# Layer 1 of a graph network: TensorE in written order around the maximum, ten pairs of values ahead of the first product, both last sums of layer 0 ahead of their norms

## The chip, the cores and the metric

The kernel runs on one core of a Trainium2 chip. The metric is the device time of one execution in microseconds (us), lower is better. The core has five engines with a queue each: TensorE (PE in the profile, its weight loads PEld), VectorE (DVE), ScalarE (ACT), GpSimd (POOL) and SyncE (SP), which here issues nearly all DMAs.

## The reference, cut to what matters

Four layers work on 3125 nodes of 128 values and 103125 edges; each ends with `x = layernorm(x + layer(x))`.

```python
x = _layernorm(x + _L0_gnn_ref(...))   # relu(segment_sum(w * (x @ W)[src], dst) + b)
x = _layernorm(x + _L1_gnn_ref(...))   # attention over edges, 4 heads of 32 values
x = _layernorm(x + _L2_gnn_ref(...))   # attention with q, k, v
x = _layernorm(x + _L3_gnn_ref(...))   # two mean aggregations
```

Layer 1, for each head, with h = x @ W:

```python
a_s = einsum('nhc,hc->nh', h, att_src); a_d = einsum('nhc,hc->nh', h, att_dst)
e = leaky_relu(a_s[src] + a_d[dst], 0.2)
p = exp(e - segment_max(e, dst)[dst]); z = segment_sum(p, dst)
out = segment_sum(h[src] * (p / z[dst]), dst) + gat_bias + x @ skip_W + skip_b   # then a layer norm
```

## The kernel before

The graph is turned into dense matrices of 25 x 25 blocks of 128 x 128: the summed edge weights in DRAM as `wd` (f32), the edge counts as `ctd` (bf16). Gathers and segment sums are then products on TensorE.

**Layer 0.** For each of 25 blocks i of source nodes, `adds0` (L840) loads the block row of `wd` with SyncE (`cw`, L847) and records products with `xw` (L851). `rows` and `todo` add the first 20 destination blocks (Z0 = 20) into five banks `acc0`. The other five blocks go into two banks, `left0` (four blocks) and `left1` (one), `acc1` in the program: rows 0 to 5 early (L1024), and rows 6 to 24 (ZA = 6) as "left rows", by `add0` (L857) in the loop `for i in range(NB)`. `end0` (L861) closes a bank: one sum with relu (L863), then the layer norm (L816): four bn_stats (L822), four aggregates (L824), small steps, a root on ScalarE (L827) and four scalings on ScalarE (L833).

**The start of layer 1.** While the left rows are summed, the finished blocks are prepared in groups of four:
- `scores1(g)` (L1280) transposes the group (`turned`, four transposes, L1042), copies it to `xT` (ScalarE L546 or VectorE L548, in turn), multiplies with the attention vectors per block (`tr_sa`, L1287) and for the row of destination scores (`tr_ad`, L1294); ScalarE copies this row out (L1296) and SyncE stores it in DRAM (L1297).
- `top` (L1401) takes the maximum of the source scores over the first eight blocks: `heads` copies the scores (L1303), a transpose on TensorE (`few`, L1076), a reduction and a small step on VectorE, and a second product on TensorE that spreads it over the partitions (L1085). From it `factors` makes the exponentials (ScalarE L1317 to L1320).
- `values(b)` (L1336) makes the values of one pair of blocks: two products (`trw`, L1341), two multiplications on VectorE (L1346), a split into three bf16 parts (`split3`, L562: VectorE L566 and L568, three casts on ScalarE, L564, L567 and L569), and a negation (L1357) into `vp`. The products `trw` use two banks in turn. `more_values` (L1407) calls it for the next pair.

The dictionary `marks` says in which step i of the loop which of these is recorded. Eight pairs (blocks 0 to 15) and the masks of column blocks 0, 1 and 2 are recorded in the loop.

**The products of layer 1.** `items` runs over two groups of destination blocks (12 and 13), four heads and 25 column blocks c. `masks` (L1370) loads the counts `ct` (L1380) and makes the mask `cm`: mostly a relu on ScalarE (L1388) and a minimum on VectorE (L1392), for some c one step on VectorE (L1384). `products` (L1456) issues two matmuls for each destination block: counts (L1464) and mask (L1468) with `vp`. A block c needs its values and its mask. The six accumulators of a head include the banks of `left0` and `left1`. The remaining pairs are recorded in this loop, as c comes near them (`ready <= c + 4`).

**What sets the order.** Each engine works through its own queue in order. Where the program says nothing, a scheduler at build time interleaves the recorded instructions by priority. `tc.manual_schedule(engines=...)` keeps the recorded order on the engines it names for the instructions recorded inside it, while the scheduler may still put others between them. `tc.issue_after(ins)` places what is recorded inside it behind `ins`, on the same engine. In the loop over `items`, the masks made in the first three steps stand behind `added`, the last sum of layer 0 (`end0` returns it).

Of the kernel before, what the change touches and what calls it, by code (L numbers as in the profile page):

```python
# [13 lines left out]
OP = mybir.AluOpType  # L14
# [486 lines left out]
ZA = 6  # L501
# [18 lines left out]
def fast_path(  # L520
# [4 lines left out]
    nc = tc.nc  # L525
# [9 lines left out]
    x = cst.tile([P, NB, P], F32, name="f_x")  # L535
# [37 lines left out]
    lp0 = ctx.enter_context(tc.tile_pool(name="f_lp0", bufs=2))  # L573
# [242 lines left out]
    def layer_norm(lp, o, i, blocks, scalar=False):  # L816

        b0, n = blocks
        bs = lp.tile([P, n, 6], F32, name="bs")
        mv = lp.tile([P, n, 2], F32, name="mv")  # L820
        for b in range(n):
            nc.vector.bn_stats(bs[:, b, :], i[:, b0 + b, :])  # L822
        for b in range(n):
            nc.vector.bn_aggr(mv[:, b, :], bs[:, b, :])  # L824
        sd = lp.tile([P, n], F32, name="sd")
        nc.vector.tensor_scalar(sd, mv[:, :, 1], EPS, None, OP.add)
        nc.scalar.activation(sd, sd, AF.Sqrt)  # L827
        nc.vector.reciprocal(sd, sd)
        if scalar:
            ms = lp.tile([P, n], F32, name="ms")  # L830
            nc.vector.scalar_tensor_tensor(ms, mv[:, :, 0], -1.0, sd, OP.mult, OP.mult)
            for b in range(n):
                nc.scalar.activation(  # L833
                    o[:, b0 + b, :], i[:, b0 + b, :], AF.Identity, bias=ms[:, b : b + 1], scale=sd[:, b : b + 1]
                )
            return
        for b in range(n):
            nc.vector.tensor_scalar(o[:, b0 + b, :], i[:, b0 + b, :], mv[:, b, 0:1], sd[:, b : b + 1], OP.subtract, OP.mult)
# [18 lines left out]
    def add0(*args):  # L857
        for f in adds0(*args):
            f()

    def end0(acc, b0, n):  # L861
        i = x[:, b0 : b0 + n, :]
        added = nc.vector.scalar_tensor_tensor(i, acc[:, 0:n, :], 0.0, i, OP.max, OP.add)  # L863
        layer_norm(lp0, i, i, (0, n), True)
        return added

    zp = front.enter_context(tc.tile_pool(name="f_zp", bufs=4))
    sp = front.enter_context(tc.tile_pool(name="f_stg", bufs=2))
# [63 lines left out]
    order = None  # L932
# [4 lines left out]
    for b in range(NBT):  # L937
# [65 lines left out]
        if b == 2:  # L1003
# [4 lines left out]
            order = ExitStack()  # L1008
# [3 lines left out]
    left = GB[Z0 // 4 :]  # L1012
    acc1 = [zpp.tile([P, 4, P], F32, name=f"left{k}") for k in range(len(left))]
# [241 lines left out]
    with ExitStack() as st:  # L1255
# [21 lines left out]
        for g in range(Z0 // 4):  # L1277
            end0(acc0[g], *GB[g])
# [28 lines left out]
        def factors(b0, n):  # L1307
            b = slice(b0, b0 + n)
            kb = km[:, None, :].to_broadcast([P, n, H])
            ta = fp.tile([P, NB, H], F32, name="ta", bufs=1)[:, 0:n]  # L1310
            nc.vector.tensor_tensor(ta, sa[:, b, 0:H], kb, OP.subtract)
            u = fp.tile([P, NB, H], F32, name="u", bufs=1)[:, 0:n]
            nc.vector.tensor_tensor(u, sa[:, b, H:], kb, OP.add)
            e = fp.tile([P, 2, NB, H], F32, name="e", bufs=1)[:, :, 0:n]
            nc.vector.tensor_scalar(e[:, 0], u, 0.8, 0.0, OP.mult, OP.min)
            nc.vector.tensor_scalar(e[:, 1], u, -0.8, 0.0, OP.mult, OP.min)
            nc.scalar.activation(fa[:, 0, b], ta, AF.Exp)  # L1317
            nc.scalar.activation(fa[:, 1, b], ta, AF.Exp, scale=0.2)
            nc.scalar.activation(own1[:, b], ta, AF.Exp, scale=-0.8)
            nc.scalar.activation(fb[:, :, b], e, AF.Exp)  # L1320
            nc.vector.tensor_scalar(fa[:, 1, b], fa[:, 1, b], -1.0, None, OP.mult)

            nc.vector.tensor_tensor(own1[:, b], own1[:, b], fb[:, 1, b], OP.mult)
            nc.vector.tensor_tensor(own1[:, b], own1[:, b], fb[:, 0, b], OP.max)
            nc.gpsimd.tensor_tensor(self_[:, b, :, C], own1[:, b], fa[:, 0, b], OP.mult)
            split3(
                fp, lambda k: of_v(b, k).rearrange("p a (s c) -> p a s c", c=F1)[:, :, :, C],
                fa[:, :, b].rearrange("p s b h -> p (b h) s"), [P, n * H, 2], "fs", [P, 12 * H, 2],
            )
            v = vp[:, b].rearrange("p b h k c -> p (b h) k c")  # L1330
            nc.vector.tensor_scalar(v[:, :, :, 2 * F1 + C], v[:, :, :, F1 + C], -1.0, None, OP.mult)
# [4 lines left out]
        def values(b):  # L1336

            n = min(2, NB - b)
            t = zps.tile([P, 2, P], F32, name="trw2", tag=f"acc{b // 2 % 2}")
            for k in range(n):  # L1340
                nc.tensor.matmul(t[:, k, :], xT[:, (b + k) * P : (b + k + 1) * P], l1_wt, start=True, stop=True)  # L1341
            h_ = t[:, 0:n].rearrange("p b (h c) -> p b h c", c=C)
            b = slice(b, b + n)
            v = fp.tile([P, 2, H, 2, C], F32, name="v")[:, 0:n]
            for s in range(2):
                nc.vector.tensor_tensor(  # L1346
                    v[:, :, :, s, :], h_, fa[:, s, b, :, None].to_broadcast([P, n, H, C]), OP.mult
                )
            nc.gpsimd.tensor_tensor(
                self_[:, b, :, 0:C], v[:, :, :, 0, :], own1[:, b, :, None].to_broadcast([P, n, H, C]), OP.mult,  # L1350
            )
            split3(
                fp, lambda k: of_v(b, k).rearrange("p a (s c) -> p a s c", c=F1)[:, :, :, 0:C],
                v.rearrange("p b h s c -> p (b h) s c"), [P, n * H, 2, C], "vs", [P, 2 * H, 2, C],
            )
            v = vp[:, b].rearrange("p b h k c -> p (b h) k c")
            nc.vector.tensor_scalar(v[:, :, :, 2 * F1 : 2 * F1 + C], v[:, :, :, F1 : F1 + C], -1.0, None, OP.mult)  # L1357
# [12 lines left out]
        def masks(g, h, c):  # L1370
            i0, n = IG[g]
            if c == 0:
                adr = dp.tile([P, GN * P], F32, name="adr")
                nc.sync.dma_start(
                    adr[:, : n * P],
                    bass.AP(tensor=add_.tensor, offset=add_.offset + h * NP + i0 * P, ap=[[0, P], [1, n * P]]),
                )
                adrs[g, h] = adr
            ct = cp.tile([P, GN * P], BF16, name="ct1")
            nc.sync.dma_start(ct[:, : n * P], ctd[c, :, i0 * P : (i0 + n) * P])  # L1380
            m = mp.tile([P, GN * P], BF16, name="cm")
            if c % 5 == 4 and (h == 0 or c == 14):
                with behind_sum(c):
                    pins["v"] = nc.vector.scalar_tensor_tensor(  # L1384
                        m[:, : n * P], adrs[g, h][:, : n * P], nas[:, c, h : h + 1], ct[:, : n * P], OP.is_gt, OP.mult
                    )
            else:
                pins["a"] = nc.scalar.activation(  # L1388
                    m[:, : n * P], adrs[g, h][:, : n * P], AF.Relu, bias=bas[:, c, h : h + 1], scale=UP
                )  # L1390
                with behind_sum(c):
                    pins["v"] = nc.vector.tensor_tensor(m[:, : n * P], m[:, : n * P], ct[:, : n * P], OP.min)  # L1392
            whole = not (h > 0 and c % 5 == 1)
            if not whole:
                pins["v"] = nc.vector.tensor_tensor(ct[:, : n * P], ct[:, : n * P], m[:, : n * P], OP.subtract)  # L1395
            ready_[g, h, c] = (ct, m, whole)
# [10 lines left out]
        def more_values():  # L1407
            nonlocal ready
            values(ready)
            ready += 2  # L1410
# [8 lines left out]
        marks[ZA + 6] = lambda: scores1(4)  # L1419
        marks[ZA + 7] = lambda: (more_values(), heads(t8, 8, Z0 - 8))  # L1420
        marks[ZA + 8] = lambda: factors(8, Z0 - 8)
        for i in (15, 17, 20, 22):
            marks[i] = more_values
        for i in range(NB):
            if i >= ZA:
                add0(cp, i, acc1, (Z0, NB - Z0), "ct1")
            if i in marks:
                marks[i]()
            if i in (19, 21, 23):
                masks(*items[(i - 19) // 2])  # L1430
# [3 lines left out]
        later(7, lambda: factors(Z0, NB - Z0))  # L1434

        for g, (b0, n) in enumerate(left):
            added = end0(acc1[g], b0, n)

        def in_range():

# [101 lines left out]
        acc = None  # L1542
        for x_, (g, h, c) in enumerate(items):
            i0, n = IG[g]
            if c == 0:
                acc = [zps.tile([P, 512], F32, name="acc1", tag=f"acc{k}") for k in ((3, 4, 2), (0, 3, 4, 2))[g]]
# [107 lines left out]
    with ExitStack() as st:  # L1654
# [108 lines left out]
        acc = None  # L1763
        for x_, (q, c) in enumerate(items):
            i0, n = QG[q]
            if c == 0:
                acc = [ap.tile([P, 512], F32, name=f"acc2_{k}") for k in range((n + 2) // 3)]
# [51 lines left out]
    with ExitStack() as st:  # L1819
# [7 lines left out]
        for g in range(3, len(GB)):  # L1827
            b0, n = GB[g]
# [3 lines left out]
        acc = [ap.tile([P, 512], F32, name=f"acc3_{k}") for k in range(len(CN))]  # L1832
# [64 lines left out]
        for k in range(K + 3):  # L1897
            if k < K:
                c, n = CN[k]
# [221 lines left out]
```

## Time and profile before

| what | value |
|---|---|
| median of 3 runs | 1296.39 us (1295.44 to 1298.28) |
| profiled execution | 1297.9 us |
| its span, first to last instruction | 1296.1 us |
| mean granted TensorE clock | 0.99 |
| TensorE busy | 1232.1 us, 95% of the span |
| VectorE busy | 955.0 us, 74% |
| ScalarE busy | 864.9 us, 67% |

Times in lines of the profile are microseconds from the start of the span. A line of a timeline has the start, the duration, the engine, the line of the program, the operation, out<-in, the shape and how many; in brackets the idle time before it and what ended it. A line of windows has, for each engine, the busy time and the number of instructions, then the granted TensorE clock, the DMA share and GB/s. An f32 matmul appears as two MATMUL records. A busy TensorE need not be at its peak, since matmuls are pipelined.

### The profile page before, as it was taken

To read this page: it belongs to the slowest core of one execution; us is meant where nothing else is said; L and a number is where in the kernel's file an instruction comes from. 1 tells how busy PE (TensorE), PEld (TensorE's weight loads), DVE (VectorE), ACT (ScalarE), POOL (GpSimd) and SP (SyncE) were. 2 spreads that over 40 slices of the span, in tenths; PEclk is the share of its full clock that TensorE was granted. 3 is DMA by queue.
4 is the path that set the end of the run, shared out by engine and by line. 5 is a ranking of instruction groups with operands and counts; after the bars stand their busy time and mean duration, and the time that the engine had idled before them with its cause. 6 is when DMAs were issued, how large, how long until landed. Compare 5 with 4: busy or idle time off the path is not lost.

```text
span 1296.1 us, 31070 instructions
## 1 busy us (share of the span) xinstructions
PE 1232.1 (95%) x13022; PEld 1100.1 (85%) x13022; DVE 955.0 (74%) x1461; ACT 864.9 (67%) x1374; POOL 149.4 (12%) x161
## 2 busy tenths in 40 slices
PE   3989999999999999999999999999999999999996
PEld 3889999999998889999999897777787778876785
DVE  6989989999925998998999987944464437332365
ACT  2977778787744997998789886534474444543454
POOL 6100000000002212230223232000000000000011
PEclk9999999999999999999999999999999999999999
DMA  7589899998997767888878775522222223861674
GB/s 186 144 234 285 240 266 279 281 275 258 286 306 248 265 197 230 281 281 257 274 252 264 210 253 190 179 74 64 62 78 74 77 63 114 262 194 49 208 209 146
DMA packets 189347, 262.37 MB, mean 202 GB/s; under 512 B 10604, under 2 KB 132763, under 8 KB 189069
## 3 DMA queue, kind: packets, MB, share of 16 engines
q1 hardware_dynamic: 188172, 257.85, 65.2%
q8 instruction: 104, 1.70, 0.5%
q0 software_dynamic: 720, 1.97, 0.5%
q10 hardware_dynamic: 305, 0.48, 0.2%
q14 instruction: 46, 0.38, 0.1%
HBM read 197.14 MB, written 63.12 MB: 201 GB/s over the span
## 4 chain that ended last, share of the span: by engine, by line
PE 69%; DVE 12%; DMA 8%; ACT 6%; issue 3%; POOL 1%; SPq 1%; POOLq 0%; ACTq 0%; DVEq 0%
PE acc L1731 9%; PE acc L1468 9%; PE s L1723 8%; PE wp L960 8%; PE acc L851 7%; PE acc L1464 5%; PE acc L1836 5%; DMA wd<-ws 5%; PE cp L952 4%; PE acc L1918 4%; DVE cm L1392 3%; ACT cm L1388 2%; DMA ct<-f_ctd 2%; DVE e L1727 1%; ACT wod L741 1%
## 5 line engine op out<-in xcount | busy, mean ns | idle before, releaser
L1464 PE MATMUL acc<-vp,ct 128*128 128x99 bf16 (+1 forms) x2500 | 323.4, 209 | 7.1 <-DVE vp L1357 5.2
L1468 PE MATMUL acc<-vp,cm 128*128 128x198 bf16 (+1 forms) x2500 | 325.2, 244 | 2.3 <-DVE cm L1392 2.0
L1388 ACT ACTIVATE cm<-adr,bas 128x1536 bf16<-128x1536 f32 (+1 forms) x184 | 287.2, 1619 | 28.5 <-PE acc L1468 19.9
L1468 PEld LDWEIGHTS <-cm 128*128 128x128 bf16 x2500 | 240.2, 97 | 13.4 <-issue 8.7
L1464 PEld LDWEIGHTS <-ct 128*128 128x128 bf16 x2500 | 242.7, 98 | 1.2 <-DVE ct L1395 0.8
L1392 DVE TENSOR_TENSOR cm<-cm,ct 128x1536 bf16<-128x1536 bf16 (+1 forms) x184 | 199.4, 1109 | 21.4 <-ACT cm L1388 19.8
L1726 ACT ACTIVATE e<-s,f_nm 128x512 f32<-128x512 f32 (+2 forms) x175 | 109.7, 633 | 114.9 <-PE s L1723 110.5
L1727 DVE TENSOR_TENSOR e<-e,ct 128x512 f32<-128x512 f32 (+2 forms) x175 | 107.7, 622 | 99.4 <-ACT e L1726 94.5
L960 PE MATMUL wp<-wod,ohc 128*128 128x128 f16 x2512 | 168.8, 220 | 2.4 <-DVE wod L908 2.2
L1731 PEld LDWEIGHTS acc<-self__6345,e 128*128 128x128 f32 x1250 | 147.5, 192 | 19.4 <-issue 10.5
L908 DVE TENSOR_TENSOR wod<-ohd,w 128x4096 f16<-128x4096 f16 (+1 forms) x82 | 155.6, 1939 | 0.0
L960 PEld LDWEIGHTS <-ohc 128*128 128x128 f16 x2512 | 150.1, 99 | 0.9 <-issue 0.3
L851 PE MATMUL acc<-f_xw,cw 128*128 128x128 f32 x1000 | 145.3, 286 | 2.8 <-DMA cw<-wd 2.8
L1731 PE MATMUL acc<-self__6345,e 128*128 128x129 f32 x1250 | 147.8, 275 | 0.0
L1723 PE MATMUL s<-yT,f_xT 128*128 128x512 f32 (+2 forms) x350 | 140.2, 538 | 1.2 <-DVE f_xT L548 1.1
L851 PEld LDWEIGHTS acc<-f_xw,cw 128*128 128x128 f32 x1000 | 125.5, 195 | 3.2 <-DMA cw<-wd 3.2
L1645 ACT CAST cr<-ct 128x1590 fp32r<-128x1590 bf16 (+3 forms) x51 | 72.3, 1418 | 77.5 <-PE acc L1836 38.1
L741 ACT COPY ws<-wp 125x512 f32<-125x512 f32 x157 | 91.2, 581 | 43.4 <-DMA wd<-ws 33.7
L741 ACT CAST cs<-cp 128x500 bf16<-128x500 f32 x157 | 91.5, 583 | 29.8 <-PE cp L952 23.8
L952 PE MATMUL cp<-ohc,ohd 128*128 128x125 f16 x1256 | 96.2, 220 | 11.6 <-ACT ws L741 11.5
L1723 PEld LDWEIGHTS s<-yT,f_xT 128*128 128x128 f32 x350 | 62.9, 190 | 49.6 <-issue 20.8
L741 ACT ACTIVATE wod<-ohd,wt 128x128 f16<-128x128 f16 x312 | 104.6, 401 | 0.0
(349 smaller groups left out, 1518.7 us busy)
## 6 DMA issues: line engine op xcount, KB each, us to landing
ct<-f_ctd SPq DMA_DIRECT2D x186, 384.0 KB
ct<-f_ctd SPq DMA_DIRECT2D x100, 416.0 KB
wd<-ws SPq DMA_DIRECT2D x39, 896.0 KB
cw<-wd SPq DMA_DIRECT2D x50, 640.0 KB
f_ctd<-cs SPq DMA_DIRECT2D x10, 2000.0 KB
ct<-f_ctd SPq DMA_DIRECT2D x25, 397.2 KB
ct<-f_ctd SPq DMA_DIRECT2D x22, 397.5 KB
ct<-f_ctd SPq DMA_DIRECT2D x25, 269.5 KB
```

The source lines that it names most:

```text
L741: line.append(f(*a, **k))
L851: steps.append(lambda j=j, a=cw[:, j - h, :]: nc.tensor.matmul(accs[j // 4][:, j % 4, :], a, xw[:, i, :], start=(i == 0 and j % 4 == 0), s ...
L908: tip[s] = nc.vector.tensor_tensor(packed(f, ww), packed(ohd, ww), twos(w2[s])[:, ww], OP.mult)
L952: nc.tensor.matmul(cp[:, j, 0:KW], ohd[:, w, :], ohc[:, w, 0:KW], start=(j == 0 and q == 0), stop=(j == 3 and q == 1), skip_group_check=True,)
L960: tip["made"] = made = nc.tensor.matmul(wp[:, j, :], ohc[:, w, :], wod[s][:, w, :], start=(j == 0 and q == 0 and s == 0), stop=(j == 3 and ...
L1388: pins["a"] = nc.scalar.activation(m[:, : n * P], adrs[g, h][:, : n * P], AF.Relu, bias=bas[:, c, h : h + 1], scale=UP)
L1392: pins["v"] = nc.vector.tensor_tensor(m[:, : n * P], m[:, : n * P], ct[:, : n * P], OP.min)
L1464: nc.tensor.matmul(out_(F1, w), ct[:, k * P : (k + 1) * P], vp[:, c, h, :, 2 * F1 : F1 + w], start=(c == 0 and k % 2 == 0), stop=False, sk ...
L1468: pins["p"] = nc.tensor.matmul(out_(0, z), m[:, k * P : (k + 1) * P], vp[:, c, h, :, 0:z], start=False, stop=(c == NB - 1 and (k % 2 == 1 ...
L1723: nc.tensor.matmul(s[:, :m], xT[:, c * P : (c + 1) * P], yT[:, i0 * P + a : i0 * P + a + m], start=True, stop=True)
L1727: masked2.append(nc.vector.tensor_tensor(e[:, a : a + m], e[:, a : a + m], ct[:, a : a + m], OP.mult))
L1731: nc.tensor.matmul(acc[k // 3][:, (k % 3) * (P + 1) : (k % 3 + 1) * (P + 1)], es[q, c][:, k * P : (k + 1) * P], vo[:, c, 0 : P + 1], start ...
```

## The change

Three things are changed, and no arithmetic. The steps i = ZA - 1 to ZA + 3 of the loop (the scores of groups 0 and 1, the maximum, the first factors, the first two pairs, the scores of group 2, and four left rows) are recorded under `manual_schedule` for TensorE. Pairs of values are recorded in steps 19, 21 and 23 instead of 20 and 22, and one more behind the last sum, so that ten pairs instead of eight stand ahead of the first product. The sum of `end0` becomes a function `add_acc`; the two sums of `left0` and `left1` come first, and both layer norms after them. `added` is still the sum of `left1`.

```diff
     def end0(acc, b0, n):
         i = x[:, b0 : b0 + n, :]
-        added = nc.vector.scalar_tensor_tensor(i, acc[:, 0:n, :], 0.0, i, OP.max, OP.add)
+        add_acc(acc, b0, n)
         layer_norm(lp0, i, i, (0, n), True)
-        return added
+
+    def add_acc(acc, b0, n):
+        i = x[:, b0 : b0 + n, :]
+        return nc.vector.scalar_tensor_tensor(i, acc[:, 0:n, :], 0.0, i, OP.max, OP.add)
...
-        for i in (15, 17, 20, 22):
+        for i in (15, 17, 19, 21, 23):
             marks[i] = more_values
+        order = ExitStack()
         for i in range(NB):
+            if i == ZA - 1:
+                order.enter_context(tc.manual_schedule(engines={mybir.EngineType.PE}))
+            if i == ZA + 4:
+                order.close()
             if i >= ZA:
                 add0(cp, i, acc1, (Z0, NB - Z0), "ct1")
...
         for g, (b0, n) in enumerate(left):
-            added = end0(acc1[g], b0, n)
+            added = add_acc(acc1[g], b0, n)
+        with tc.issue_after(added.ins):
+            more_values()
+            for b0, n in left:
+                i = x[:, b0 : b0 + n, :]
+                layer_norm(lp0, i, i, (0, n), True)
```

## The prediction

> **What bounds the kernel now.** I read the page first: one core, TensorE busy nearly always. So a change is worth what it does to TensorE's idle time and clock, in its own stage.
>
> ```profile
> span 1296.1 us, 31070 instructions
> PE 1232.1 (95%) x13022; PEld 1100.1 (85%) x13022; DVE 955.0 (74%) x1461; ACT 864.9 (67%) x1374; POOL 149.4 (12%) x161
> ```
>
> Then the windows around the edit. 403.7 is the last product of layer 0's first 20 blocks; 441.4 is the first product of layer 1; the last value is ready at 489.8.
>
> ```profile
> core 0: us, PE busy (x) PEld busy (x) DVE busy (x) ACT busy (x) POOL busy (x), PEclk, DMA share, GB/s
> 403.70:415.50 11.80, 11.56 (x86) 9.30 (x86) 5.78 (x33) 9.07 (x23) 4.53 (x7) 1.00 0.76 253
> 415.50:441.40 25.90, 25.90 (x212) 23.40 (x211) 23.34 (x56) 21.85 (x42) 8.99 (x14) 1.00 0.73 244
> 441.40:463.00 21.60, 20.20 (x270) 18.37 (x269) 18.89 (x48) 19.73 (x31) 4.58 (x7) 1.00 0.71 239
> 463.00:476.00 13.00, 12.80 (x185) 12.60 (x182) 13.00 (x20) 12.93 (x15) 1.23 (x2) 1.00 0.78 223
> 476.00:491.00 15.00, 9.97 (x139) 9.45 (x138) 14.92 (x27) 12.70 (x16) 2.42 (x3) 1.00 0.65 180
> 491.00:494.50 3.50, 3.50 (x31) 3.30 (x29) 1.41 (x3) 0.00 (x0) 0.00 (x0) 0.51 0.37 144
> 494.50:550.00 55.50, 55.44 (x870) 55.21 (x869) 51.14 (x55) 50.20 (x34) 14.92 (x11) 1.00 0.81 265
> ```
>
> To 441.4 TensorE is full. From 463 to 491 VectorE is full, and TensorE loses 5.0 us waiting; then comes half clock (0.51). From 494.5 TensorE is full again, so a delay before 494.5 goes to the end. The waits say for what:
>
> ```profile
> engine line waited for: us in total, times, longest us
> PE acc L1464 <- DVE vp L1357: 5.2, 4, 2.4
> PE acc L1464 <- DVE f_x L863: 1.4, 2, 0.7
> PE tr_sa L1287 <- ACT f_xT L546: 0.2, 1, 0.2
> ```
>
> The timeline splits the 5.2 us into 0.20 (pair 16), 1.55 (18), 1.05 (20), 2.43 (22). TensorE and VectorE around the maximum, and VectorE at layer 0's last sum:
>
> ```profile
> 403.73 1.04 PE L1042 MATMUL tr<-f_ident,f_x 128*128 128x128 f32 x8
> 405.01 1.06 PE L1287 MATMUL tr_sa<-watt,f_xT 128*128 128x8 f32 x8 [0.24 <-ACT f_xT L546]
> 413.18 0.27 PE L1076 MATMUL few<-f_ident,ex 128*4 128x128 f32 x1
> 414.30 0.39 PE L1085 MATMUL few<-d_all,ones 128*128 128x4 f32 x2
> ```
>
> ```profile
> 446.55 0.26 DVE L863 SCALAR_TENSOR_TENSOR f_x<-left,f_x 128x128 f32<-128x128 f32 x1
> 446.72 0.16 DVE L826 TENSOR_SCALAR sd<-mv 128x4 f32<-128x4 f32 x1
> 446.79 0.95 DVE L1392 TENSOR_TENSOR cm<-cm,ct 128x1536 bf16<-128x1536 bf16 x1
> ```
>
> **The change, part by part.** Times below are from the start of the span. The order of the changed program on each queue is known from its build; I follow it with durations of the old trace. Slots, by start to start: a transpose 0.11, a group's four 0.44; tr_sa of a group 0.89; tr_ad 0.95; a row of five left products 1.12; a pair's two trw 0.45; two products (L1464 and L1468) 0.134. A copy of xT costs 0.20 from the transpose to its start, 0.59 (ScalarE) or 0.69 (VectorE), and 0.05 to TensorE.
>
> (1) TensorE in order. Before, eight transposes stood ahead of tr_sa, and left products filled each wait. Now:
> - Group 0's four transposes end at 404.17; its tr_sa starts at 405.01 as before, behind the copy. The other four no longer fill: +0.44. With tr_ad it ends at 406.95.
> - Group 1: transposes to 407.39; its copy is on VectorE, so tr_sa starts at 407.39 + 0.20 + 0.69 + 0.05 = 408.33: +0.94. With tr_ad and one left row TensorE is at 411.29.
> - The written order covers five steps only. The scheduler has put seven transposes and tr_ad of groups 3 and 4, which belong to later steps, ahead of the maximum's transpose. Group 3's four end at 411.73, its copy is with TensorE at 412.67, the other three transposes end at 412.06: +0.61. After tr_ad, the maximum's transpose (L1076) runs at 413.62, against 413.18 before. It is not earlier, so VectorE's longest wait here (3.63, for L1076) does not become a gain.
> - The second product of the maximum comes 1.12 behind the first before; one left row fills this: 0.
> - Group 2: its transposes now come after the maximum; 0.84 for the ScalarE copy less one transpose that fills: +0.73.
>
> Sum 2.7. From there left rows stand between pairs; every pair's input is old by then: 0, bounds 0 to 1. ScalarE's table load (1.28) has an idle ScalarE ahead of it: 0.
>
> (2) Ten pairs instead of eight ahead of the first product: four trw, 0.89. First product 441.42 + 2.7 + 0.9 = 445.0. The 0.89 is missing later, so net 0.
>
> (3) The masks. VectorE per pair, from start to start: two L1346 0.67, L566 0.60, L568 0.60, L1357 0.28, together 2.15; ScalarE three casts of 0.52, 1.57. Before, only a 0.07 step stood between the last sum (446.55) and the mask of column block 3 (L1392, 446.79).
> Where is that sum now? Ahead of it come half of pair 8 (L1346 twice, L566: +1.27); behind it go the norm's four L822 and four L824 (-1.04) and a L1357 (-0.28): 0 together. But TensorE now starts pairs 0 to 3 at 416.2, 420.9, 424.5 and 429.0, against 412.62, 416.79, 419.90 and 424.96, and VectorE had read pair 1 at once (its wait for trw L1341 was 1.3) and pair 2 and 3 within 2 us. So it idles more: between 0 and 2.5, and I take the middle, 1.3: 447.8.
> Between the sum and the mask now stand two L1357 0.56, two L1346 0.67, L568 0.60, L566 0.60, five L822 0.93, four L824 and a L826 0.31: 3.7. The mask runs from 451.6, TensorE has it at 452.7. TensorE is through three blocks at 445.0 + 36 x 0.134 + 0.3 = 450.1: it waits 2.6. Block 4's mask is VectorE's own (L1384, 1.80, behind 0.67): ready at 455.1, while TensorE is through block 3 at 454.3: 0.8. Later blocks: 0.1. Sum +3.5; bounds 1.5 (VectorE earlier by 1.3 and quicker through its queue by 0.7) and 5 (later by 1.2, with waits on ScalarE).
>
> (4) Both sums ahead of the norms: the products wait for the two banks, 1.4 before. TensorE comes there at 447, the sums end at 447.8: 0.3 stays, -1.1. The norms move back by some 4 us; their result is used by the last score groups, whose values are due at block 20: 0.
>
> (5) The waits for values. Pairs 16 and 18 are now ahead: -1.75. Pairs 20 to 24 stand where they stood; their waits (1.05 + 2.43) vanish only as far as TensorE is later than the vector work. TensorE is late at block 6 by 2.7 + 0.9 + 3.5 - 1.1 = 6.0, less 0.89 and 1.75: 3.35. ScalarE: the mask of block 5 started at 447.36; now it stands behind pair 9's last cast, which needs L568 (ends 453.2): 453.8, 6.4 late, less the two pairs' casts (3.14) that are now done: 3.3. Both are equally late, so the 3.5 us stay: 0; bounds -3.5 and +2.
>
> (6) SyncE's loads of left rows and of ct share eight buffers and follow TensorE's left products, so ct is issued some 3.6 us later. Block 3's was issued at 436.3 for a use at 446.8, and the use moves by 4.8: 0; without that cover 3.6. The store of group 3's scores now stands ahead of group 2's, both ahead of the row load that the first mask reads: 0 for it, 0.3 at most. GpSimd's steps have 4.5 of 11.8 us busy: 0; without that cover, 0.6 for each L1349.
>
> Sum: 2.7 + 3.5 - 1.1 - 1.75 = +3.35.
>
> The clock: the 0.51 row is some 3.4 us at half clock, a loss of 1.7. It follows waits of 1.05 and 2.43. After has such a wait at 450 and again near 490. I count one such stretch as before (0); bounds -1.7 and +3.4.
> The Trainium skill ("TensorE: Matmul & The Clock Gate", Why this matters for your kernels) puts the drop behind idle gaps of over about 3 us. The longest wait ahead of the 0.51 row is 2.43, so row and page differ, and the row decides. By the page no wait of after would slow the clock, and the sum would be 1.7 lower, 1298.0.
>
> **Against the time.** The profiled execution took 1297.9 (span 1296.1 and 1.8 around it); + 3.35 is 1301.3. The median of the runs lies 1.5 below it; for the median: 1296.4 + 3.35 = 1299.7.
>
> **The rivals.** What a measurement of this kernel can tell from no change is 0.2%, 2.6 us.
> - *Faster.* The masks of blocks 3 and 4 come in time, because VectorE does the two pairs inside the idle 8.6 us it has from 403.7 to 441.4. Then part 3 costs 0, all 5.2 of the waits go and with them the half clock: 2.7 - 1.1 - 5.2 - 1.7 = -5.3, 1291.1. It decides where the mask of block 3 ends before 450.1. For it: 3.63 of that idle time is the wait for the maximum. Against it: the maximum's transpose is not earlier in the new order, and pairs 8 and 9 come from TensorE only at 443 to 445. Chance 0.1.
> - *No change.* As forecast, but the wait near 490 is short enough to keep the clock: 3.35 - 1.7 = +1.65, 1298.0; or (5) gains 1 to 3. Chance 0.3.
> - *Slower still.* Half clock behind the early waits, and behind both late ones: +1.7 to +3.4 more, 1301.4 to 1303.1. Against it: 1.4 us in two waits at 444 to 447 left the clock at 1.00. Chance 0.12.
> - *The order written is not what runs*: it is so in part (the seven transposes), and in the sum already.
>
> **How the numbers follow.** Forecast 1299.7 (0.48 for +2.6 to +4.4). Faster 0.1, same 0.3, slower 0.48 + 0.12 = 0.6. The range leaves out the faster rival and the ends: 1295.8 (+3.35 less 3.5, the bound of part 5, rounded for the spread of the runs) to 1302.8.
>
> **What would show it.** Right: L1076 at 413 to 414; first layer 1 product at 444 to 446; TensorE waiting 2 to 4 us for DVE cm L1392 and L1384 near 450 to 455; waits for vp L1357 down from 5.2 to about 3. Wrong: L1076 before 412, no wait for cm, or the waits for vp gone.

## The result, and the profile after

The changed kernel takes a median of 1300.86 us (1296.77 to 1304.97, 12 runs), the kernel before 1296.62 (1290.74 to 1300.09, 12 runs, the same chip): the ratio is 1.0034, with a 95% interval of 1.0018 to 1.0051. The forecast was 1299.7, in a range of 1295.8 to 1302.8. It is slower, by a little more than forecast. The profiled execution took 1301.22 (span 1299.3), against 1297.9 (span 1296.1).

The page first: the first row of the span and the busy times.

```profile
span 1299.3 us, 31079 instructions
PE 1232.7 (95%) x13022; PEld 1099.8 (85%) x13022; DVE 954.8 (73%) x1461; ACT 865.8 (67%) x1374; POOL 151.9 (12%) x161
```

The work is the same (13022 matmul records, busy 0.6 us more); of the 3.2 us, 2.6 are idle time of TensorE. The view of waits of TensorE from 403 to 500 us says for what (total, times, longest):

```profile
PE acc L1477 <- DVE vp L1360: 2.8, 2, 2.2
PE acc L1481 <- DVE cm L1395: 2.6, 1, 2.6
PE trw L1344 <- DVE v L1349: 1.3, 1, 1.3
PE tr_sa L1290 <- ACT f_xT L546: 1.2, 2, 0.7
PE tr_sa L1290 <- DVE f_xT L548: 0.8, 1, 0.8
PE tr_ad L1297 <- DVE f_xT L548: 0.5, 1, 0.5
PE acc L1477 <- DVE f_x L868: 0.4, 2, 0.3
```

Lines of the changed kernel lie 3 to 13 further down: L863 is now L868, L1357 is L1360, L1392 is L1395, L1464 is L1477. The waits for values fell from 5.2 to 2.8, those for the last sums from 1.4 to 0.4. New are three more waits for copies of xT (2.2 more in all), one for a mask (2.6), and one that the prediction did not have: a pair's product (trw) waits 1.3 for VectorE to read the bank. The timeline of TensorE shows the order in which they come, from the first transpose to the first product of layer 1 and the mask:

```profile
404.50 0.60 PE L1045 MATMUL tr<-f_ident,f_x 128*128 128x128 f32 x4
405.78 1.06 PE L1290 MATMUL tr_sa<-watt,f_xT 128*128 128x8 f32 x8 [0.68 <-ACT f_xT L546]
...
409.16 1.06 PE L1290 MATMUL tr_sa<-watt,f_xT 128*128 128x8 f32 x8 [0.79 <-DVE f_xT L548]
...
413.70 1.02 PE L1297 MATMUL tr_ad<-f_xT,watt 128*4 128x512 f32 x2 [0.46 <-DVE f_xT L548]
414.65 0.27 PE L1079 MATMUL few<-f_ident,ex 128*4 128x128 f32 x1
...
418.94 1.06 PE L1290 MATMUL tr_sa<-watt,f_xT 128*128 128x8 f32 x8 [0.56 <-ACT f_xT L546]
...
446.76 0.68 PE L1344 MATMUL trw<-f_l_wt,f_xT 128*128 128x128 f32 x4 [1.34 <-DVE v L1349]
447.28 0.21 PE L1477 MATMUL acc<-vp,ct 128*128 128x102 bf16 x1
...
455.90 0.26 PE L1481 MATMUL acc<-vp,cm 128*128 128x198 bf16 x1 [2.63 <-DVE cm L1395]
```

And VectorE's timeline from the last sum to the mask of column block 3. Before, 0.24 us lay between them; now the vector work of the two late pairs and half the norm does, 3.99 us, with no idle time in it:

```profile
450.90 0.28 DVE L868 SCALAR_TENSOR_TENSOR f_x<-left,f_x 128x128 f32<-128x128 f32 x1
451.10 0.35 DVE L1360 TENSOR_SCALAR vp<-vp 128x768 bf16<-128x768 bf16 x1
...
454.83 0.15 DVE L826 TENSOR_SCALAR sd<-mv 128x4 f32<-128x4 f32 x1
454.89 0.95 DVE L1395 TENSOR_TENSOR cm<-cm,ct 128x1536 bf16<-128x1536 bf16 x1
```

**How kernels are compared below.** The profiled spans of this study differ already ahead of the change: the first transpose lay between 399.1 and 409.1 us. So the stage is measured from its own first transpose (L1042 before). Four times are taken: the maximum's transpose; the first product of layer 1; "product 288" (counted from 0, the first of the last column block of the first head, behind the last wait for values); and VectorE's idle time ahead of the first product (length less busy in the windows row). The windows rows of before and after, from first transpose to first product to product 288:

```profile
core 0: us, PE busy (x) PEld busy (x) DVE busy (x) ACT busy (x) POOL busy (x), PEclk, DMA share, GB/s
403.73:441.42 37.69, 37.45 (x298) 32.68 (x297) 29.11 (x88) 30.91 (x63) 13.52 (x21) 1.00 0.74 247
441.42:494.51 53.09, 46.46 (x616) 43.73 (x614) 48.20 (x94) 45.33 (x59) 8.23 (x12) 0.97 0.69 212
```

```profile
404.50:447.28 42.78, 38.96 (x306) 33.44 (x305) 31.73 (x93) 32.28 (x64) 13.99 (x23) 1.00 0.73 236
447.28:498.93 51.65, 45.67 (x608) 42.76 (x606) 45.47 (x88) 44.61 (x56) 7.58 (x11) 0.97 0.64 203
```

Ahead of the first product the change costs 5.1 us (42.78 against 37.69), behind it it gives 1.4 back (51.65 against 53.09): +3.65 at product 288, and +3.66 at product 600. The clock is 0.97 in both second rows: one half-clock stretch each. The span's +3.2 is this, +0.77 ahead of the first transpose, and -1.2 late in the span, mainly because a half-clock stretch that before shows at 726.6 us is not there in after.

| kernel | maximum's transpose | first product | product 288 | VectorE idle ahead of first product | half clock, 440 to 500 us | ratio to before, 95% interval |
|---|---|---|---|---|---|---|
| before | 9.44 | 37.68 | 90.77 | 8.6 | 491.0 | 1 |
| changed | 10.15 | 42.78 | 94.42 | 11.1 | 456.7 | 1.0034 (1.0018 to 1.0051) |
| order_only | 10.15 | 40.31 | 93.87 | 11.6 | 493.2 | 1.0016 (0.9999 to 1.0032) |
| ten_pairs_only | 9.74 | 38.87 | 90.85 | 7.9 | 447.2 | 0.9987 (0.9967 to 1.0008) |
| sums_first_only | 9.44 | 37.68 | 90.71 | 7.6 | none | 0.9989 (0.9971 to 1.0008) |
| no_order | 9.44 | 38.58 | 91.42 | 7.6 | 450.7 | 1.0001 (0.9982 to 1.0021) |
| masks_first | 9.45 | 38.58 | 92.68 | 7.6 | 491.8 | 1.0008 (0.9995 to 1.0022) |
| neg_after | 10.15 | 41.96 | 97.35 | 10.1 | 452.1, 493.1 | 1.0050 (1.0031 to 1.0068) |
| copies_covered | 16.14 | 45.29 | 98.12 | 16.0 | 461.2 (and 410.0) | 1.0070 (1.0052 to 1.0087) |
| max_early | 14.50 | 52.50 | 104.87 | 21.3 | 466.0 (and 407.9, 431.8) | 1.0081 (1.0063 to 1.0099) |
| early_eight | 8.87 | 41.60 | 94.24 | 10.6 | 492.8 | 1.0017 (0.9999 to 1.0035) |
| early_ten | 8.87 | 41.52 | 92.01 | 9.1 | none | 1.0009 (0.9994 to 1.0025) |
| early_changed | 8.87 | 41.77 | 94.35 | 9.1 | 492.6 | 1.0031 (1.0013 to 1.0048) |
| early_ten_bank | 6.94 | 38.53 | 89.05 | 5.8 | none | 0.9993 (0.9980 to 1.0006) |

The expectations below count every VectorE record as busy and so give its idle time as 7.0 (before) and 10.5 (changed); the table's 8.6 and 11.1 are the windows rows.

A half-clock stretch ahead of product 288 is part of that column. In before, the 24 products from the end of the last wait (489.68) to product 288 take 4.83 us with the stretch in them; in sums_first_only, which has none, the same 24 take 3.19. So a stretch weighs about 1.6 us there. Three kernels of the table have none ahead of product 288 (sums_first_only, early_ten, early_ten_bank); the first four comparisons of the change (before, changed, order_only, no_order) have one each.

### The profile page after: what moved, and what is told of

The parts are those of the page before. It is cut to its first block, busy times and chain, and to the rows that moved or that the text cites. A ratio compares the mean times of both kernels' runs of the same rounds, so it can differ in the third digit from the quotient of the medians.

```text
span 1299.3 us, 31079 instructions
## 1 busy us (share of the span) xinstructions
PE 1232.7 (95%) x13022; PEld 1099.8 (85%) x13022; DVE 954.8 (73%) x1461; ACT 865.8 (67%) x1374; POOL 151.9 (12%) x161
## 4 chain that ended last, share of the span: by engine, by line
PE 67%; DVE 14%; DMA 9%; ACT 5%; issue 4%; POOL 1%; SPq 0%; DVEq 0%; POOLq 0%; ACTq 0%
PE acc L1744 9%; PE acc L1481 8%; PE s L1736 8%; PE wp L963 8%; PE acc L851 7%; DMA wd<-ws 6%; PE acc L1849 5%; PE acc L1477 5%; PE cp L955 4%; PE acc L1931 4%; DVE cm L1395 3%; DMA ct<-f_ctd 1%; PE left L851 1%; ACT cm L1391 1%; DVE e L1740 1%
## 5 line engine op out<-in xcount | busy, mean ns | idle before, releaser
L1477 PE MATMUL acc<-vp,ct 128*128 128x99 bf16 (+1 forms) x2500 | 321.0, 208 | 3.7 <-DVE vp L1360 2.8
L1477 PEld LDWEIGHTS <-ct 128*128 128x128 bf16 x2500 | 241.4, 97 | 1.1 <-DVE ct L1398 0.6
L1395 DVE TENSOR_TENSOR cm<-cm,ct 128x1536 bf16<-128x1536 bf16 (+1 forms) x184 | 198.8, 1106 | 21.2 <-ACT cm L1391 17.7
L1744 PEld LDWEIGHTS acc<-self__6345,e 128*128 128x128 f32 x1250 | 147.5, 192 | 19.4 <-issue 10.5
```

Source lines behind the costliest of these rows:

```text
L1477: nc.tensor.matmul(out_(F1, w), ct[:, k * P : (k + 1) * P], vp[:, c, h, :, 2 * F1 : F1 + w], start=(c == 0 and k % 2 == 0), stop=False, sk ...
L1744: nc.tensor.matmul(acc[k // 3][:, (k % 3) * (P + 1) : (k % 3 + 1) * (P + 1)], es[q, c][:, k * P : (k + 1) * P], vo[:, c, 0 : P + 1], start ...
```

## The experiments

**Each part by itself.** Four kernels split the change.

order_only: the kernel before, and at the loop over i

```diff
+        order = ExitStack()
         for i in range(NB):
+            if i == ZA - 1:
+                order.enter_context(tc.manual_schedule(engines={mybir.EngineType.PE}))
+            if i == ZA + 4:
+                order.close()
```

> The kernel before with one of the three parts: TensorE in the written order for steps 5 to 9; eight pairs, sums and norms as before. Theory (each part does what the prediction gave it): TensorE loses 2.7 us to uncovered copies around the maximum, the first layer 1 product starts at 444 to 445 (before 441.4) and its mask is not late, since no pair and no norm is moved; the waits for values shrink by at most 2.7 from 5.2, so the time is 0 to 2.7 us above before, ratio 1.000 to 1.002. Rival (the written order is the whole loss): the change's +3.2 us are all here, ratio 1.0025 to 1.0034. Rival (the half-clock stretch decides, not the order): the stretch at 491 us goes and with it 1.7 us, ratio 0.9985 to 1.000.

Measured: first product 2.63 later than before, product 288 3.10 later, ratio 1.0016 (0.9999 to 1.0032). TensorE's waits for copies:

```profile
PE tr_sa L1287 <- ACT f_xT L546: 1.2, 2, 0.7
PE tr_sa L1287 <- DVE f_xT L548: 0.8, 1, 0.8
PE tr_ad L1294 <- DVE f_xT L548: 0.5, 1, 0.5
```

These are the changed kernel's four waits for copies, 2.24 us more than before's 0.24, and most of the first product's 2.63. The waits for values stay at 5.0: later TensorE did not mean shorter waits, so the vector work came as much later. Nearly the whole loss of the stage is here, a little more than the theory's bound of 2.7, as the first rival has it; the ratio lies in the theory's range, and its interval reaches into both. The half-clock stretch did not go, and the second rival falls.

ten_pairs_only: the kernel before, and

```diff
-        for i in (15, 17, 20, 22):
+        for i in (15, 17, 19, 21, 23):
...
             added = end0(acc1[g], b0, n)
+        with tc.issue_after(added.ins):
+            more_values()
```

> The kernel before with one of the three parts: ten pairs of values ahead of the first product (marks 15, 17, 19, 21, 23 and one call behind the last sum); the norms stay where they were, and TensorE's order is the scheduler's. Theory: the first product is 0.9 us later (442.3), VectorE's mask of column block 3 stands behind the two late pairs' vector work and TensorE waits 1 to 3 us for a mask between 446 and 455; the waits for values fall from 5.2 to 3.5 or less; together +0.5 to +2, ratio 1.0004 to 1.0015. Rival (the two late pairs' work fits into VectorE's idle time from 404 to 441): no wait for a mask, 1.8 us less in waits for values, ratio 0.998 to 0.999.

Measured: product 288 at 90.85, as before (90.77); ratio 0.9987 (0.9967 to 1.0008), no difference that can be told. Waits for values fell from 5.2 to 2.3, those for masks rose from 0 to 1.8 and for the sums from 1.4 to 2.0. The theory's +0.5 to +2 was too high: what is moved ahead comes back in about the same size. The rival's ratio was met, but not its reason: a mask is waited for.

sums_first_only: the kernel before, with `add_acc` twice and then both layer norms, behind the last sum.

> The kernel before with one of the three parts: both last sums of layer 0 ahead of both norms, and the norms behind the last sum; eight pairs, TensorE's order the scheduler's. Theory: the products' waits for the two accumulators' banks fall from 1.4 to at most 0.3 us, the mask of column block 3 now has five L822, four L824 and one L826 ahead of it (1.2 us) but its ready time stays ahead of TensorE or costs at most 0.5 us; the waits for values stay 4 to 6 us, since VectorE has the same work before them; together -1.1 to +0.5, ratio 0.999 to 1.0005. Rival (the moved norms are what makes the mask late): a wait for DVE cm of 1 to 2.6 us, ratio above 1.0008.

Measured: product 288 at 90.71, ratio 0.9989 (0.9971 to 1.0008). The waits for sums fell only to 1.1, those for values rose to 6.2, and no mask is late: the moved norms alone do not make a mask late. But this trace has no half-clock stretch in the stage; at the clock of before, product 288 would be some 1.6 us later, about 92.3 (an estimate, from the 24 products above).

no_order: the changed kernel less the five lines of order_only.

> The changed kernel without the written order on TensorE: ten pairs ahead and both sums ahead of the norms stay. Theory (TensorE in order makes 2.7 to 3.5 of the first product's 5.9 us of delay, and the masks the rest of the loss): first product 442 to 443.5, a wait for a mask of block 3 or 4 of 2 to 4 us (VectorE's queue behind the last sum is as long as in the changed kernel, and TensorE comes earlier), waits for values 2 to 4 us; +0 to +2 against before, ratio 1.000 to 1.0015. Rival (the written order is the whole loss, the other parts gain): -1 to -3 us, ratio 0.9977 to 0.9992. Rival (the written order costs nothing that lasts, the queue of VectorE decides): as the changed kernel, +3 to +4, ratio 1.0023 to 1.0034.

Measured: product 288 at 91.42, +0.65 against before and 3.00 below the changed kernel; ratio 1.0001 (0.9982 to 1.0021).

```profile
PE acc L1472 <- DVE vp L1360: 3.3, 2, 2.2
PE acc L1476 <- DVE cm L1395: 2.3, 1, 2.3
PE acc L1472 <- DVE f_x L868: 1.4, 1, 1.4
```

The theory held. The late mask is there (2.3) without the written order, and the time is that of before. So the written order makes about 3 of the 3.65 us, alone (3.10) and together with the other two parts (3.00), and these two make 0.65. All four traces have one half-clock stretch in the stage, so the clock has little part in these differences.

**Does a late mask cost anything by itself?** masks_first: no_order, with the mask of block 3 recorded right behind the last sum.

```diff
         with tc.issue_after(added.ins):
+            masks(*items[3])
             more_values()
...
-        made = 3
+        made = 4
```

> The changed kernel without the written order, and with the mask of column block 3 recorded ahead of the tenth pair and of the norms, right behind the last sum. Theory (VectorE is full, and its queue only decides for what TensorE waits): the wait for the mask of block 3 (2.35 us without the written order) falls to at most 0.8, the waits for values (3.3) or for later masks rise by about as much, and the 288th product stays within 1 us of 91.4 after the first transpose; ratio to before 0.999 to 1.001. Rival (the late mask is a loss by itself, as the prediction's third step had it): the wait goes and the others stay, the 288th product 2 to 2.5 us earlier, ratio 0.997 to 0.9985.

```profile
PE acc L1473 <- DVE vp L1360: 2.9, 2, 2.2
PE acc L1477 <- DVE cm L1387: 2.7, 1, 2.7
PE acc L1473 <- DVE f_x L868: 1.4, 1, 1.4
PE acc L1477 <- DVE cm L1395: 0.7, 1, 0.7
```

The wait for the mask of block 3 (2.35 in no_order) is gone; the mask of block 4 (L1387, VectorE's own) and that of block 8 (L1395), never late in no_order, are now 2.7 and 0.7 late. Product 288 is 1.26 later, a little outside the theory's 1 us, and the rival's 2 to 2.5 us earlier fails. The half-clock stretch is also elsewhere (491.8 in place of 450.7), so this kernel alone does not say how much of the 1.26 is waits (7.9 in all, against 7.2). It says that the waiting moves on to other masks.

**Work taken off VectorE.** neg_after: the changed kernel, and in `values`

```diff
-            nc.vector.tensor_scalar(v[:, :, :, 2 * F1 : 2 * F1 + C], v[:, :, :, F1 : F1 + C], -1.0, None, OP.mult)
+            nc.gpsimd.tensor_scalar(v[:, :, :, 2 * F1 : 2 * F1 + C], v[:, :, :, F1 : F1 + C], -1.0, None, OP.mult)
```

> The changed kernel with one step of every pair of values taken off VectorE: the negation of the high half of vp (0.28 us on VectorE from start to start, thirteen pairs) is issued on GpSimd, which is busy for 4 to 5 of 12 us there. Theory (VectorE's queue sets the end of the stage): VectorE has 3.6 us less to do, the waits for the mask and for values (2.6 and 2.8) fall by 2 to 4 us in all, and the 288th product comes 2 to 3.5 us earlier after the first transpose than in the changed kernel (94.4); ratio to before 1.000 to 1.002. Rival (TensorE's waits in the written order set it): no change, 1.003 to 1.0035. Rival (GpSimd's step is slow and each product waits for it): waits for POOL vp of 1 us or more, ratio above 1.004.

The second rival (a slow GpSimd step) held: ratio 1.0050 (1.0031 to 1.0068), product 288 at 97.35. From GpSimd's timeline, two of these steps in a row, and the last two; then the product that waits for them on TensorE:

```profile
440.31 4.77 POOL L1360 TENSOR_SCALAR vp<-vp 128x768 bf16<-128x768 bf16 x2 [2.17 <-ACT vp L569]
490.89 3.59 POOL L1360 TENSOR_SCALAR vp<-vp 128x768 bf16<-128x768 bf16 x2 [2.17 <-ACT vp L569]
```

```profile
493.40 0.25 PE L1477 MATMUL acc<-vp,ct 128*128 128x102 bf16 x1 [4.66 <-DMA ct<-f_ctd]
```

GpSimd takes 2.1 to 3.6 us for a step (twelve of 128x768) where VectorE took 0.28, from start to start. The wait of 4.66 is put down to a load, but ends at 493.40, just behind the first of the two GpSimd steps that end the row above (490.89, at most 2.46): the releaser named had long been done. The test was meant to tell whether VectorE's queue or TensorE's own waits set the end of the stage, and with so slow a step it does not.

**Can the written order be filled?** Six kernels keep a written order and fill it by hand. copies_covered: the changed kernel, with the transposes a step ahead of their score products, and so a left row over each copy; max_early: the written order goes on to step 13 as well.

```diff
-        marks = {ZA - 1: lambda: [scores1(g) for g in range(2)], ZA: top}
+        marks = {ZA - 1: lambda: [turned1(g) for g in range(2)], ZA: lambda: ([scores1(g, False) for g in range(2)], top())}
...
```

> The changed kernel; in the written order of the same five steps the transposes of groups 0, 1 and 2 are recorded one step earlier than their score products, so that a row of left products stands between a group's transposes and the product that waits for their copy. Theory (the written order costs what its uncovered copies cost): TensorE's waits for the copies of xT (0.67, 0.79, 0.46 and 0.56 us in the changed kernel) fall to 0.5 us in all, the maximum's transpose comes 9 to 9.7 us after the first transpose (changed kernel 10.15), the first product 39 to 40.5 us after it (changed kernel 42.8, without the order 38.6); the time is 1.5 to 3 us below the changed kernel, ratio to before 1.000 to 1.002. Rival (the loss is TensorE's later wait for VectorE to read a pair's bank and the late masks, not the copies): first product at 41.5 or later, ratio to before 1.0025 or more.

> The same as the kernel before it in this list, and the written order goes on for four more steps, so that the score products of groups 3 and 4 can't be put ahead of the maximum. Theory (VectorE's queue sets the end of this stage, and the written order cost it 3.5 us of idle time ahead of the first product: 10.5 against 7.0): the maximum's transpose comes 6 to 7 us after the first transpose (before 9.45), VectorE's wait for it falls from 3.6 to under 1.5, its idle time ahead of the first product to 4 to 6 us, and the 288th product comes 1 to 4 us earlier after the first transpose than before (90.8); ratio to before 0.997 to 0.9995. Rival (TensorE's own waits set it, an earlier maximum gives nothing): the 288th product at 90.5 to 92, ratio 1.000 to 1.001. Rival (the written order costs whatever it holds, since the scheduler's filling is lost): ratio 1.002 or more.

Both theories were far off: 1.0070 (1.0052 to 1.0087) and 1.0081 (1.0063 to 1.0099). The ratios are those of the rivals that had the loss stay, but for a reason that none of them named. In copies_covered no copy is waited for any more, but TensorE's timeline has

```profile
405.04 1.04 PE L1045 MATMUL tr<-f_ident,f_x 128*128 128x128 f32 x8
408.59 1.35 PE L851 MATMUL left<-f_xw,cw 128*128 128x128 f32 x10 [2.52 <-DMA cw<-wd]
409.78 1.51 PE L1295 MATMUL tr_sa<-watt,f_xT 128*128 128x8 f32 x8
411.22 1.87 PE L1302 MATMUL tr_ad<-f_xT,watt 128*4 128x512 f32 x2
```

The row that was to fill had not landed: SyncE, which had waited for TensorE, issued its load only 0.2 us after the first transpose (405.23), and the products started 3.4 us later (408.59). The wait of 2.52 is followed by 10.2 us at half clock (410.0 to 420.2): tr_ad takes 1.80 in place of 0.96, start to start. max_early waited 3.37 there and had 13.7 us at half clock, and later 2.17 for a copy of xT, with another stretch behind it (431.8). The scheduler's order asks for two products of that row at 3.6 us and for the rest from 5.9.

(`turned1` is the first lines of `scores1`, the transposes and their copy, made a function.) early_eight, early_ten and early_changed cover the copies with other groups' transposes instead, ask for the first row at 5.7 us, and keep groups 3 and 4 behind the maximum (the order is in the first expectation); they differ in the pairs and norms.

```diff
+        marks = {ZA - 1: lambda: (turned1(0), turned1(1), scores1(0, False), turned1(2), scores1(1, False))}
+        marks[ZA] = lambda: (top(), turned1(3))
...
-            if i == ZA + 4:
+            if i == ZA + 8:
```

> The kernel before (eight pairs, norms as they were) with a written order on TensorE for steps 5 to 13 that is filled by hand: transposes of groups 0 and 1, scores of group 0, transposes of group 2, scores of group 1, a left row, the maximum's transpose, transposes of group 3, a left row, the maximum's product, a left row, pair 0, scores of group 2 and so on. Each copy of xT has other work over it, no left row is asked for within 5 us of the first transpose (its load landed 3.5 us after it where a row was placed too early), and groups 3 and 4 are behind the maximum. Theory (the written order as such costs nothing; its uncovered waits do, and an earlier maximum takes idle time off VectorE): maximum's transpose 6 to 7 us after the first transpose (before 9.45), VectorE's idle time ahead of the first product 3 to 5 us (before 7.0), waits for values 1 to 3.5 us (before 5.2); 288th product 87.5 to 90 us after the first transpose (before 90.8); ratio 0.997 to 0.9995. Rival (TensorE has 0.9 us less to fill with and waits elsewhere; VectorE's idle time only moves): 288th product 90.5 to 92.5, ratio 1.000 to 1.002.

> The same written order with ten pairs of values ahead of the first product, norms as they were. Theory: as with eight pairs in VectorE's idle time; the first product 38.6 us after the first transpose, the wait for a mask (1.8 us with ten pairs and no written order) and the waits for values (2.3) fall by 1.5 to 3 us in all; 288th product 87.5 to 90 us; ratio 0.996 to 0.999. Rival: 288th product 90.5 to 93, ratio 1.000 to 1.002.

> The changed kernel with the written order filled by hand as in the two kernels before it in this list (ten pairs, both sums ahead of the norms). Theory: 288th product 88 to 91 us after the first transpose against 94.4 in the changed kernel, the wait for the mask of block 3 (2.6) 0 to 1.5, no wait of 0.4 us or more for a copy of xT; ratio to before 0.997 to 1.000. Rival (the loss of the changed kernel is not in the uncovered copies and the late maximum): 288th product 92.5 or later, ratio 1.002 or more.

The theories failed: product 288 at 94.24, 92.01 and 94.35, ratios 1.0017, 1.0009 and 1.0031, those of the rivals (early_eight's product 288 is even beyond its rival's 92.5, and early_ten's 92.01 is without a half-clock stretch). Ahead of the first product the copies are waited for by 0.24 in all; in each of the three two new waits stand in their place, here in early_ten:

```profile
411.15 0.27 PE L1076 MATMUL few<-f_ident,ex 128*4 128x128 f32 x1 [1.76 <-ACT ad L1301]
442.14 1.38 PE L851 MATMUL left<-f_xw,cw 128*128 128x128 f32 x10 [0.80 <-DMA cw<-wd]
```

The maximum's tile uses the bank of group 1's tr_ad (acc1), and ScalarE, behind eight norm steps of layer 0 (L833), copied it out only at 411.1. early_ten_bank gives that tile the bank acc4:

```diff
+            spare.append(lambda: zps.tile([P, 512], F32, name="few", tag="acc4"))
             heads(t8, 0, 8)
...
-        marks[ZA + 1] = lambda: (spread(keep["d"], H, km), factors(0, 8))
+        marks[ZA + 1] = lambda: (spread(keep["d"], H, km), spare.pop(), factors(0, 8))
```

> The kernel with the hand-filled written order, ten pairs of values and the norms as before, and the two small tiles of the maximum in the bank acc4 in place of acc1, so that the maximum's transpose no longer waits for ScalarE to copy group 1's ad out of acc1 (1.76 us in the three kernels before). Theory (what the hand-filled order lost was this one wait and the late left row): the maximum's transpose 6.9 to 7.5 us after the first transpose (8.9 with acc1, 9.45 before), the first product 39.2 to 41 us after it (41.5 with acc1), VectorE's wait for the maximum under 1.2 us (2.5), the 288th product 88.5 to 91 (92.0 with acc1, before 90.8); ratio 0.997 to 1.000. Rival (the next wait takes its place: a left row that has not landed, or ScalarE's queue of norm steps, which then holds back the factors): 288th product 91.5 to 93, ratio 1.000 to 1.002.

The theory held. The maximum's transpose is at 6.94, the first product at 38.53, and product 288 at 89.05, still in a written order. That is 2.96 earlier than in early_ten, from which it differs by the bank alone, at the same clock. It is 5.4 us earlier than in the changed kernel, about 1.6 of it for want of a half-clock stretch, and its norms stand as before. The order around the maximum, and the first windows row:

```profile
403.60 1.04 PE L1042 MATMUL tr<-f_ident,f_x 128*128 128x128 f32 x8
404.87 1.06 PE L1292 MATMUL tr_sa<-watt,f_xT 128*128 128x8 f32 x8 [0.24 <-ACT f_xT L546]
405.86 1.02 PE L1299 MATMUL tr_ad<-f_xT,watt 128*4 128x512 f32 x2
406.81 0.66 PE L1042 MATMUL tr<-f_ident,f_x 128*128 128x128 f32 x4
407.38 1.06 PE L1292 MATMUL tr_sa<-watt,f_xT 128*128 128x8 f32 x8
...
410.54 0.27 PE L1076 MATMUL few<-f_ident,ex 128*4 128x128 f32 x1
```

```profile
403.60:442.13 38.53, 38.29 (x305) 33.46 (x304) 32.75 (x92) 32.43 (x64) 14.76 (x22) 1.00 0.74 246
```

TensorE waits 0.24 us in the whole row and VectorE is idle for 5.8 of it, against 8.6 before. No row is late any more. Its median is 1293.82 against 1294.49 of before on the same chip, ratio 0.9993 (0.9980 to 1.0006): below the changed kernel's interval, and not to be told from before. It is 1.72 us ahead of before at product 288. 1.6 of that is the half-clock stretch that before has and this one has not; the waits are 5.9 against 6.8, which about pays for the 0.9 of four more trw.

## Why the prediction was right, and where not

The direction and the size held, and so did the net of each half: +2.7 for the written order (measured 3.0 to 3.1 at product 288), and +0.65 for everything else (3.5 - 1.1 - 1.75; measured 0.65). The mechanism of the first half was right. That the second half came out to 0.65 is in part luck: terms inside it were mis-sized and happened to balance, and one sign that was named, the first product at 444 to 446, was missed (447.28).

- *(1) TensorE in order, 2.7.* Shown by order_only: 2.63 at the first product, by the four copies that the prediction listed; the maximum's transpose came 0.7 later (0.44 was forecast), and VectorE's idle time rose by 3.0. The 0 for what comes behind the maximum (bounds 0 to 1) failed in the changed kernel: a late pair's trw waited 1.34 for its bank. This wait is in neither order_only nor no_order, only in the changed kernel and, with 0.53, in neg_after, where VectorE is late and ten pairs go through the two banks. That the two together make it is not shown.
- *(2) Four trw, 0.89.* no_order's first product is 0.90 later than before's. With the written order it came at 42.78 after the first transpose, where the prediction's 445.0 is 41.27: 1.5 more, nearly all of it that trw.
- *(3) Masks, 3.5.* The wait was 2.63 for a forecast of 2.6, by two errors that cancel. The last sum came 46.4 after the first transpose, not 44.1 (VectorE's idle time was guessed at the middle of 0 to 2.5, and was near the end), and TensorE was 1.5 late itself. The 0.8 for block 4 did not appear. More than that, no_order has this wait and no loss of that size, and masks_first moved it to the next mask: it is not a price to be added by itself, but a place where VectorE's backlog shows.
- *(4) Both sums first, -1.1.* 0.44 of waiting stayed, 0.3 was forecast. Alone it gave nothing: in sums_first_only the waits for sums fell by only 0.3, and those for values rose by 1.0. Nor do the parts add up: ten_pairs_only is at +0.1 and sums_first_only at some +1.6 at an equal clock, both together in no_order at +0.65.
- *(5) Values.* 2.8 stayed, 3.5 was forecast; the mechanism (TensorE and vector work equally late) fits order_only, where 5.0 of 5.2 stayed.
- *(6) SyncE and GpSimd, 0.* No wait of the changed kernel names a load or GpSimd. copies_covered shows how near the loads were.
- *The clock.* One stretch in the stage, as counted, but behind the wait for the mask (456.7) and not at 491. The absent stretch at 726.6 was not foreseen, and lies far behind the stage.

The faster rival decided at a mask ready by 450.1; it was ready at 455.8. The prediction held against it that the maximum does not come earlier in the new order; early_ten_bank is the other side of that argument, an earlier maximum in a filled order.

What stays open: whether TensorE's own waits or VectorE's idle time is the cause in the written order. In three kernels they rise and fall together (early_ten_bank, before, changed: VectorE idle 5.8, 8.6, 11.1 and product 288 at 89.05, 90.77, 94.42). But no_order has 7.6 and is at 91.42, and early_ten and early_changed have 9.1 each and are at 92.01 and 94.35 (some 1.6 of this is the clock), so VectorE's idle time alone does not set product 288. The kernel that was to part the two (neg_after) did not. The medians agree with the traces, but most single ratios' intervals include 1.

## What to carry to other kernels

A hand-written order on an engine that is full is only as good as its worst uncovered wait: list, for each instruction in it, the copy, the bank and the load that it needs and when each is there, since the scheduler's order had been filling all but 0.24 us of them here. Where two engines are both nearly full, a wait that is moved comes back at the next place, so price the stage by the backlog at its end, not by the sum of the waits that you can name. And compare traces from a mark just ahead of the change, when the part ahead of it differs by more than the effect.

## What the runs showed of the hardware

- In each trace the half-clock stretches start on one grid of 3.413 us, the length of a single stretch (before: 395.46, 491.04 and 726.55, each 3.41 us long; the first two are 28 steps apart, the last two 69). What goes with them is TensorE's idle time inside one step of that grid. Between 400 and 500 us of before, the changed kernel and ten of the others (copies_covered and max_early are left out), each step with 1.95 us idle or more (1.95 to 3.41, ten of them) was followed by a half-clock stretch, and none with 1.79 or less. So the same wait may cost a stretch or not: 2.43 us before (2.06 of it in one step) did, 2.42 in sums_first_only (1.79 and 0.63) did not. Outside this part of the traces the border is less sharp: steps with 1.70 us idle (neg_after, ahead of a stretch at 390.7) and 1.79 (before, ahead of that at 726.6) were followed by a stretch, and one with 1.88 (copies_covered, from 85.8) was not. From ten_pairs_only, the step with 1.95 idle and the next one, clock in the third column from the end:

```profile
443.80:447.20 3.40, 1.45 (x21) 1.14 (x18) 3.40 (x17) 2.72 (x5) 0.61 (x1) 1.00 0.41 117
447.20:450.60 3.40, 3.40 (x29) 3.18 (x27) 2.85 (x5) 2.99 (x7) 0.21 (x1) 0.51 0.79 266
```

The Trainium skill ("TensorE: Matmul & The Clock Gate", Why this matters for your kernels) names one idle window, gaps of over about 3 us, as the cause; here a window that was a little over half idle was enough, made up of two waits (0.51 and 1.44 us).

- Behind 2.52 us of waiting, copies_covered ran 10.2 us at half clock, three steps of the grid, though its timeline shows no wait of TensorE in them. Why it took three is open.
- The negation of 128x768 bf16 that takes VectorE 0.28 us from start to start took GpSimd 2.1 to 3.6 (neg_after).
